# Gated delta rule in a fused two-layer kernel: keys and queries stay in the convolution's tiles, and their products move 128 columns

## The chip, the cores and the metric

The kernel runs on one core of a Trainium2 chip. The metric is the device time of one execution in microseconds, given as the median of several runs. Three runs of the kernel before gave 1481.29 us (1479.42 to 1482.24).

The core's engines run side by side, each with its own queue of instructions in order: PE (TensorE, matrix products, with its weight loads listed as PEld), DVE (VectorE), ACT (ScalarE, functions from tables that have to be loaded), POOL (GpSimd) and SP (which here only issues DMAs).

## The reference, cut to what matters

There are 1024 tokens of 256 features. Each of two layers mixes and then applies experts; the change touches only the first layer's attention, a chunked gated delta rule with 16 key heads and 32 value heads of 128:

```python
conv = silu(causal_conv(x @ w_qkv, conv_w))      # depthwise, four taps
q, k, v = split(conv)                            # q, k: 16 heads, v: 32 heads
q = l2norm(q); k = l2norm(k)
A = where(strict, -(k_beta @ k.T) * decay, 0)    # per chunk
attn = inverse(I - A)                            # unit lower triangular
...
attn_i = where(lower, q_i @ k_i.T * d_i, 0)
o_i = (q_i * exp(g_i)) @ state + attn_i @ v_new
out = rms_norm(core) * norm_w * silu(x @ w_z)
x = x + out @ w_out
```

For the change, what counts is this: after the convolution, silu is applied to keys and queries; the products of keys with keys and of keys with queries (the grams) are formed; and the squares of both are summed for the norm. Everything is float32.

## The kernel before

Tokens are handled in two halves (s = 0, 1) of two sequences of 256 tokens each. A unit is one key head with its two value heads in one half, so there are 32 units, named by head and half. Four units make a group. Inside a unit the 256 tokens of a sequence are two chunks (n = 0, 1) of 128, and b is the sequence.

A unit goes through these stages. In `Unit.products` (line 771) `convolved` (line 728) makes the projection with two products of 512 columns for q and for k, and ACT and DVE apply the four taps into a tile `accq` or `acck` of 128 x 512 (2 KB on each partition). ACT then writes silu into two new tiles, `kq0` and `kq1`, one for each chunk, with q and k of a chunk side by side: four activations of 256 elements. PE forms the grams (lines 795 to 819): for each of three pairs of chunks and each sequence, one product with k of one chunk as weights and the 256 columns of k and q of the other chunk moving. Two activations square `kq0` and `kq1`, and the products `kt` sum the squares over tokens. DMA brings the cumulated decay rows, and POOL and ACT make of them the decay matrix `attnT`, which POOL multiplies with the grams into the group's `X` and into `attnT`.

`Group.small_inverses` (line 482) then inverts the 32 x 32 diagonal blocks of a group's four units at once, mostly on DVE: transposes `Rt` of X, a chain of 60 small operations on `xs`, and the transposes `Tc` and `Rt_c`. `Unit.inverse` and `Group.inverse64` join the blocks with small products (`lu`, `lx`, `lxu`) and evictions by DVE and ACT. `Unit.values` convolves the values (`accv`, products `cvv`; silu is applied in place there), `Unit.outputs` runs the products `vn`, `at` and `ks`, `Unit.normed` normalizes and gates (POOL), and `Group.project` (`wo`) adds the projection to x for two units at a time. `Rest` holds everything after the attention, with the experts' products `h`, `a`, `e` and `ae`.

Nobody wrote the instruction order by hand. Every operation is recorded on a tape with an engine, an estimated cost, the tiles that it reads and writes, and sometimes a due time; `Tape.plan` (line 289) simulates the five engines and picks, in up to ten rounds, which operation each engine issues next. It knows how many tiles are free: nearly all tiles of 2 KB come from one pool of `PLACES` places (line 1439), and `MOST` (line 1441) limits how many each use may hold at once, with 4 where there is no entry. `SPARE` (lines 257 and 418) sets how many PSUM banks are kept for more urgent work, and `ENOUGH` (lines 287 and 423) sets when small products on PE are held back. So a change of the tiles, the costs or these numbers can change the order of all engines. Operations are emitted through one helper, so in the profile nearly all of them have line 128, and they are told apart by their tiles.

Of the kernel before, what the change touches and what calls it, by code (L numbers as in the profile page):

```python
# [11 lines left out]
AF = mybir.ActivationFunctionType  # L12
# [4 lines left out]
P = 128  # L17
B, T, C = 4, 256, 256
NTOK = B * T
NH = 16  # L20
# [161 lines left out]
class Tape:  # L182
# [11 lines left out]
    def op(self, engine, cost, emit, r=(), w=(), port=False, table=None, due=None, late=0.0, to=None, dense=1.0,  # L194
           few=False):

        o = Op()
        o.engine, o.cost, o.emit, o.late, o.table, o.due = engine, cost, emit, late, table, due
        o.dense, o.few = dense, few
        o.port = port or engine == "POOL"
        o.before, o.after, o.bufs = set(), [], []
        o.order = n = len(self.ops)
        for accesses, write in ((r, False), (w, True)):
            for at in accesses:
                buf, parts = at if isinstance(at, tuple) else (at, None)
                for other, its, wrote in buf.history:  # L210
                    if (write or wrote) and (parts is None or its is None or parts & its):
                        o.before.add(other)
                if write and parts is None:
                    buf.history.clear()
                buf.history.append((n, parts, write))
                if buf.bufs is not None and buf not in o.bufs:
                    o.bufs.append(buf)
                    buf.uses += 1
        for buf in to if isinstance(to, list) else [to] if to else []:
            if buf not in o.bufs:  # L220
                o.bufs.append(buf)
                buf.uses += 1
        o.before.discard(n)
        for i in o.before:
            self.ops[i].after.append(n)
        self.ops.append(o)
# [188 lines left out]
            o.emit()  # L415


ROUNDS, SWITCH, LOAD, SPARE, AHEAD, EACH, END, IDLE, MOMENT, GAP, RATE, GIVES = 10, 11.7, 1.3, 106.8, 160.0, 23.99, 1300.0, 54.95, 0.68, 66.3, 3.14, 5.0
UNIT = 42

EARLY, FEW = range(3, 5), 6
WIDE = 96
WINDOW, ENOUGH, LITTLE, SLOW, THIN = 3.4, 0.51, 0.38, 0.5, 10.0


def _mm(n, count=1):

    return count * {512: 0.86, 256: 0.43, 128: 0.222, 64: 0.149, 32: 0.05}[n]


def _act(n):
    return 0.2 + 0.00078 * n
# [252 lines left out]
class Unit:  # L685
# [85 lines left out]
    def products(self):  # L771
        p, s, h = self.p, self.s, self.h
        e, op = p.e, p.tape.op
        gate = p.gateb[s]
        w = self.load("wqk")

        kq = self.kq = [self.buf([P, 2, 2, P], "kq0", 2), self.buf([P, 2, 2, P], "kq1", 6)]
        for j, at in ((1, 0), (0, 1)):
            acc = self.convolved(w, at, at * NH + h, "qk"[j == 0])
            for n in range(2):  # L780

                def emit(n=n, j=j, acc=acc):
                    e.scalar.activation(
                        kq[n]()[:, :, j, :], acc()[:, :, n * P : n * P + P], AF.Silu
                    )

                op("ACT", _act(256), emit, [acc], [(kq[n], {j})], table="silu")


        kqm = []  # L790
# [3 lines left out]
        cost = lambda n: (engine, length(n))  # L794
        def gram(n0, n, ps):
            for b in range(2):
                e.tensor.matmul(
                    ps()[:, b * 256 : b * 256 + 256],
                    kq[n0]()[:, b, 0, :],
                    kq[n]()[:, b].rearrange("p j d -> p (j d)"),  # L800
                    start=True,
                    stop=True,
                )

        for pairs in (((0, 0),), ((1, 1), (0, 1))):
            of = []
            for n0, n in pairs:
                ps = p.ps(f"gram{n0}{n}_{self.tag}")
                m = self.buf([P, 2, 2, P], "kqm" if n0 == n else "cross", 2, name=n0)
                kqm.append(m)  # L810
                of.append((n0, n, ps, m))

            def grams(of=of):
                for n0, n, ps, _ in of:
                    gram(n0, n, ps)

            op(
                "PE",
                _mm(256, 2 * len(of)),
                grams,  # L820
                kq[: len(of)],
                [ps for _, _, ps, _ in of],
                to=[m for _, _, _, m in of],
            )
            for _, _, ps, m in of:

                def taken(m=m, ps=ps):
                    copy(
                        m().rearrange("p j b d -> p b j d"),
                        ps().rearrange("p (b j d) -> p b j d", b=2, j=2),  # L830
                    )

                op(*cost(512), taken, [ps], [m])
        self.cross = kqm[2]

        ps = p.ps(f"kt_{self.tag}")
        sums = lambda j: ps()[:, 504 + 4 * j : 508 + 4 * j]

        sqs = []
        for n in range(2):  # L840
            sq = self.buf([P, 2, 2, P], "sq", 2, name=n)
            sqs.append(sq)
            op(
                "ACT",
                _act(512),
                lambda n=n, sq=sq: e.scalar.activation(sq(), kq[n](), AF.Square),
                [kq[n]],
                [sq],
            )

        def norms(ps=ps):


            for at in reversed(range(8)):
                j, n, b = at // 4, at // 2 % 2, at % 2
                e.tensor.matmul(
                    ps()[:, 505 + at - WIDE : 505 + at],
                    sqs[n]()[:, b, j, :],
                    p.const(LT)[:, P - WIDE :],
                    start=True,  # L860
                    stop=True,
                )

        op("PE", 1.0, norms, sqs, [ps], dense=0.7)

        k2, ki = self.buf([P, 4], "k2", 3), self.buf([P, 2, 2], "ki", 3)
# [346 lines left out]
    def gates(self, early=False):  # L1213
# [18 lines left out]
        for n in range(2):  # L1232
            zs = self.buf([P, 2, 2, P], "zse" if early else "zs", 3, name=n)
            of.append(zs)
            ps = p.ps(f"z{n}_{self.tag}")

            def products(n=n, ps=ps):
                for b in range(2):
                    for k in range(2):
                        e.tensor.matmul(  # L1240
                            ps()[:, b * 256 : b * 256 + 256],
                            p.tokens(4 * s + 2 * b + n)[:, k, :],
                            wz()[:, k, :],
                            start=k == 0,
                            stop=k == 1,
                        )

            op("PE", _mm(256, 4), products, [wz, p.actb[s]], [ps], to=zs, few=early)

            def silu(zs=zs, ps=ps):  # L1250
                e.scalar.activation(
                    zs().rearrange("p v b d -> p b v d"),
                    ps().rearrange("p (b v d) -> p b v d", b=2, v=2),
                    AF.Silu,
                )

            op("ACT", _act(512), silu, [ps], [zs], table="silu")
# [97 lines left out]
class Program:  # L1355
# [80 lines left out]
            return self.place(tag, name, shape)  # L1436
        return Buf(self.tape, pool, shape, tag, f"{tag}_{name}", bufs)

    PLACES = 59

    MOST = {'attnT': 20, 'kq1': 12, 'kq0': 2, 'kqm': 16, 'cross': 10, 'vo': 8, 'zs': 6, 'oT': 6, 'w0': 6, 'hw0': 8, 'w1': 6, 'hw1': 8, 'wo': 2, 'sq': 4, 'r0': 5, 'wqk': 20, 'vn': 20, 'acck': 20, 'wb0': 12}

    def place(self, use, name, shape=(P, 512)):

        to = Buf(self.tape, self.up, list(shape), "place", f"{use}_{name}", self.PLACES)
        to.slots.in_turn = False
        to.slots.rate = RATE
        return to.queue(self.tape, use, self.MOST.get(use, 4))

# [3 lines left out]
    def ps(self, name):  # L1453
        ps = Buf(self.tape, self.psum, [P, 512], "ps", f"ps_{name}", 6)
        ps.slots.in_turn = False
        return ps
# [760 lines left out]
```

## Time and profile before

| | |
|---|---|
| median of three runs | 1481.29 us |
| the profiled execution | 1474.44 us, its span 1472.6 us |
| PE busy | 1388.6 us, 94% of the span, 8428 products |
| DVE, ACT, POOL busy | 1127.7, 932.7, 918.6 us |
| mean granted clock of PE | 0.981 |
| ACT table loads (line 128) | 114, of 1283 ns |
| moved by DMA | 128.60 MB, mean 87 GB/s |

A row of a group gives the operation, the tiles written and read, the shape, the count, the busy time with the mean time of one, and the idle time before with what ended it. A row of the timeline starts with the start and the length of a merged piece. Each float32 product of the program appears as two products in the records, each with a weight load. The ends of products are modelled and overlap with the next, so the time that one takes in a stream is read from start to start.

### The profile page before, as it was taken

To read this page: it belongs to the slowest core of one execution; us is meant where nothing else is said; L and a number is where in the kernel's file an instruction comes from. 1 tells how busy PE (TensorE), PEld (TensorE's weight loads), DVE (VectorE), ACT (ScalarE), POOL (GpSimd) and SP (SyncE) were. 2 spreads that over 40 slices of the span, in tenths; PEclk is the share of its full clock that TensorE was granted. 3 is DMA by queue.
4 is the path that set the end of the run, shared out by engine and by line. 5 is a ranking of instruction groups with operands and counts; after the bars stand their busy time and mean duration, and the time that the engine had idled before them with its cause. 6 is when DMAs were issued, how large, how long until landed. Compare 5 with 4: busy or idle time off the path is not lost.

```text
span 1472.6 us, 24086 instructions
## 1 busy us (share of the span) xinstructions
PE 1388.6 (94%) x8428; PEld 899.4 (61%) x8428; DVE 1127.7 (77%) x2117; ACT 932.7 (63%) x2013; POOL 918.6 (62%) x913
## 2 busy tenths in 40 slices
PE   4987899999999899999999999889999999999988
PEld 2655676876875686776687677654445644444433
DVE  7799898798698679889879989955785677785133
ACT  2688788888878888888888887733342742121220
POOL 3069859948754785985986875448643654664032
PEclk9998999999999899999999999999999999999999
DMA  6042122211120231222231223155332231658030
GB/s 213 10 136 76 47 77 87 83 46 41 59 73 29 74 98 62 66 73 72 66 110 50 65 54 94 44 165 157 107 105 83 73 126 55 188 155 245 0 115 14
DMA packets 80953, 128.60 MB, mean 87 GB/s; under 512 B 10160, under 2 KB 26288, under 8 KB 80832
## 3 DMA queue, kind: packets, MB, share of 16 engines
q1 hardware_dynamic: 79824, 125.91, 28.0%
q8 instruction: 67, 1.10, 0.3%
q10 hardware_dynamic: 1008, 1.16, 0.3%
q14 instruction: 54, 0.44, 0.1%
HBM read 121.36 MB, written 5.67 MB: 86 GB/s over the span
## 4 chain that ended last, share of the span: by engine, by line
PE 70%; DVE 15%; POOL 5%; ACT 4%; issue 3%; DMA 2%; SPq 0%; DVEq 0%; POOLq 0%; ACTq 0%
PE ps_wo L128 7%; PE ps_cvv L128 6%; PE ps_h L128 5%; PE ps_a L128 5%; PE ps_z L128 5%; PE ps_at L128 4%; PE ps_gram L128 4%; PE ps_ae L128 4%; PE ps_e L128 3%; PE ps_kt L128 3%; PE ps_cvk L128 3%; PE ps_cvq L128 3%; PE ps_vn L128 3%; DVE accv_v L128 2%; PE ps_mix L128 2%
## 5 line engine op out<-in xcount | busy, mean ns | idle before, releaser
L128 ACT ACT_TABLE_LOAD x114 | 146.3, 1283 | 21.5 <-DVE sb_xT L128 8.9
L128 DVE SCALAR_TENSOR_TENSOR accv_v<-ps_cvv,sb_convw,accv_v 128x510 f32<-128x510 f32 (+2 forms) x192 | 141.7, 742 | 7.2 <-ACT accv_v L128 2.2
L128 POOL TENSOR_TENSOR hw_h<-hw_h,r_h 128x512 f32<-128x512 f32 x64 | 85.9, 1348 | 77.7 <-DVE hw_h L128 76.1
L128 PE MATMUL ps_cvv<-ratio,wv 128*128 128x512 f32 x256 | 122.5, 609 | 2.3 <-DVE acck_k L128 1.3
L128 PE MATMUL ps_h<-ratio,w_w 128*128 128x512 f32 x256 | 117.7, 601 | 7.4 <-DMA w_w<-in_w 5.8
L128 ACT ACTIVATE r_h<-ps_h 128x512 f32<-128x512 f32 x64 | 38.2, 597 | 132.2 <-PE ps_h L128 129.4
L128 PE MATMUL ps_a<-hw_h,w_w 128*128 128x512 f32 x256 | 117.0, 595 | 1.6 <-POOL hw_h L128 1.6
L128 PE MATMUL ps_z<-wz,ratio 128*128 128x256 f32 x480 | 116.1, 390 | 0.4 <-ACT zs L128 0.4
L128 PE MATMUL ps_wo<-oT,wo 128*128 128x512 f32 x256 | 112.8, 593 | 0.8 <-ACT oT L128 0.8
L128 POOL TENSOR_TENSOR hw_e<-hw_e,r_e 128x512 f32<-128x512 f32 x32 | 41.5, 1312 | 92.1 <-ACT r_e L128 61.0
L128 PEld LDWEIGHTS ps_z<-wz,ratio 128*128 128x128 f32 x480 | 89.8, 194 | 14.2 <-issue 0.9
L128 POOL TENSOR_TENSOR vd<-vn,dc 128x512 f32<-128x512 f32 x32 | 34.1, 1064 | 98.3 <-ACT vn L128 97.8
L128 POOL TENSOR_TENSOR X<-attnT,kqm 128x512 f32<-128x512 f32 x64 | 83.6, 1314 | 12.4 <-ACT kqm L128 12.1
L128 PEld LDWEIGHTS ps_h<-ratio,w_w 128*128 128x128 f32 x256 | 48.5, 192 | 67.2 <-issue 59.8
L128 DVE TENSOR_TENSOR xs<-xs,prod 128x30 f32<-128x30 f32 (+14 forms) x240 | 81.2, 338 | 8.2
L128 PEld LDWEIGHTS ps_a<-hw_h,w_w 128*128 128x128 f32 x256 | 48.0, 190 | 61.5 <-issue 51.6
L128 ACT ACTIVATE junko<-vo 128x128 f32<-128x128 f32 x256 | 79.4, 310 | 7.3
L128 PEld LDWEIGHTS ps_wo<-oT,wo 128*128 128x128 f32 x256 | 48.1, 190 | 58.7 <-issue 53.1
L128 DVE TENSOR_TENSOR prod<-xs,Rt 128x30 f32<-128x30 f32 (+14 forms) x240 | 78.8, 328 | 6.4
L128 POOL TENSOR_TENSOR attnT<-attnT,kqm 128x512 f32<-128x512 f32 x64 | 82.6, 1303 | 1.5
L128 DVE SCALAR_TENSOR_TENSOR hw_h<-ps_h,wb_wb 128x512 f32<-128x512 f32 x64 | 43.8, 684 | 51.8 <-ACT r_h L128 39.2
L128 PE MATMUL ps_at<-vn,attnT 128*128 128x128 f32 x512 | 82.1, 276 | 0.0
(258 smaller groups left out, 3764.1 us busy)
## 6 DMA issues: line engine op xcount, KB each, us to landing
attnT<-G SPq DMA_DIRECT2D x64, 256.0 KB, 4.9
w_w<-in_w SPq DMA_DIRECT2D x64, 256.0 KB, 4.4
wb_wb<-w_rows SPq DMA_DIRECT2D x128, 128.0 KB, 3.3
wqk<-in_wqk SPq DMA_DIRECT2D x32, 256.0 KB, 2.9
wv<-in_wv SPq DMA_DIRECT2D x32, 256.0 KB, 3.6
wo<-in_wo SPq DMA_DIRECT2D x32, 256.0 KB, 3.0
qe<-G SPq DMA_DIRECT2D x32, 256.0 KB, 3.6
wz<-in_wz SPq DMA_DIRECT2D x30, 256.0 KB, 2.7
```

Of the source, the lines that this page charges most:

```text
L128: return self._tc.keep_in_program_order(f(*a, **k))
```

## The change

Silu is applied in place in `accq` and `acck`, each with one activation of 512 elements, and the tiles `kq0` and `kq1` are gone. A chunk of q or k is now a slice of such a tile; since k and q of a chunk no longer lie side by side, a gram that moved 256 columns becomes two that move 128 each, with the same weights loaded for both. The squares are taken of q and of k instead of chunk by chunk, with the same count and size, and the sums read them accordingly. The pool grows from 59 to 61 places, three uses get an entry in `MOST`, and two numbers of the planner change.

```diff
-ROUNDS, SWITCH, LOAD, SPARE, AHEAD, EACH, END, IDLE, MOMENT, GAP, RATE, GIVES = 10, 11.7, 1.3, 106.8, 160.0, 23.99, 1300.0, 54.95, 0.68, 66.3, 3.14, 5.0
+ROUNDS, SWITCH, LOAD, SPARE, AHEAD, EACH, END, IDLE, MOMENT, GAP, RATE, GIVES = 10, 11.7, 1.3, 57.48, 160.0, 23.99, 1300.0, 54.95, 0.68, 66.3, 3.14, 5.0
...
-WINDOW, ENOUGH, LITTLE, SLOW, THIN = 3.4, 0.51, 0.38, 0.5, 10.0
+WINDOW, ENOUGH, LITTLE, SLOW, THIN = 3.4, 0.53, 0.38, 0.5, 10.0
...
-        kq = self.kq = [self.buf([P, 2, 2, P], "kq0", 2), self.buf([P, 2, 2, P], "kq1", 6)]
+        kq = [None, None]
         for j, at in ((1, 0), (0, 1)):
-            acc = self.convolved(w, at, at * NH + h, "qk"[j == 0])
-            for n in range(2):
-
-                def emit(n=n, j=j, acc=acc):
-                    e.scalar.activation(
-                        kq[n]()[:, :, j, :], acc()[:, :, n * P : n * P + P], AF.Silu
-                    )
-
-                op("ACT", _act(256), emit, [acc], [(kq[n], {j})], table="silu")
+            acc = kq[j] = self.convolved(w, at, at * NH + h, "qk"[j == 0])
+            op(
+                "ACT",
+                _act(512),
+                lambda acc=acc: e.scalar.activation(acc(), acc(), AF.Silu),
+                [],
+                [acc],
+                table="silu",
+            )
+
+        def chunk(j, n, b):
+            return kq[j]()[:, b, n * P : n * P + P]
...
             for b in range(2):
-                e.tensor.matmul(
-                    ps()[:, b * 256 : b * 256 + 256],
-                    kq[n0]()[:, b, 0, :],
-                    kq[n]()[:, b].rearrange("p j d -> p (j d)"),
-                    start=True,
-                    stop=True,
-                )
+                for j in range(2):
+                    at = (2 * b + j) * P
+                    e.tensor.matmul(
+                        ps()[:, at : at + P],
+                        chunk(0, n0, b),
+                        chunk(j, n, b),
+                        start=True,
+                        stop=True,
+                    )
...
-                _mm(256, 2 * len(of)),
+                _mm(128, 4 * len(of)),
                 grams,
-                kq[: len(of)],
+                kq,
...
-        for n in range(2):
-            sq = self.buf([P, 2, 2, P], "sq", 2, name=n)
+        for j in range(2):
+            sq = self.buf([P, 2, T], "sq", 2, name=j)
...
-                lambda n=n, sq=sq: e.scalar.activation(sq(), kq[n](), AF.Square),
-                [kq[n]],
+                lambda j=j, sq=sq: e.scalar.activation(sq(), kq[j](), AF.Square),
+                [kq[j]],
...
-                    sqs[n]()[:, b, j, :],
+                    sqs[j]()[:, b, n * P : n * P + P],
...
-    PLACES = 59
+    PLACES = 61
...
-    MOST = {'attnT': 20, 'kq1': 12, 'kq0': 2, 'kqm': 16, 'cross': 10, 'vo': 8, 'zs': 6, 'oT': 6, 'w0': 6, 'hw0': 8, 'w1': 6, 'hw1': 8, 'wo': 2, 'sq': 4, 'r0': 5, 'wqk': 20, 'vn': 20, 'acck': 20, 'wb0': 12}
+    MOST = {'attnT': 20, 'kq1': 12, 'kq0': 2, 'kqm': 16, 'cross': 10, 'vo': 8, 'zs': 6, 'oT': 6, 'w0': 6, 'hw0': 8, 'w1': 6, 'hw1': 8, 'wo': 2, 'sq': 4, 'r0': 5, 'wqk': 20, 'vn': 20, 'acck': 20, 'wb0': 12, 'qe': 2, 'wv': 8, 'state': 16}
```

## The prediction

> **What bounds the kernel now.** I read the totals of the page first, then the chain of work that ended last, then busy time by stretches, then the tensor engine's timeline where a stretch was not full.
>
> ```profile
> PE 1388.6 (94%) x8428; PEld 899.4 (61%) x8428; DVE 1127.7 (77%) x2117; ACT 932.7 (63%) x2013; POOL 918.6 (62%) x913
> PEclk9998999999999899999999999999999999999999
> ...
> PE 70%; DVE 15%; POOL 5%; ACT 4%; issue 3%; DMA 2%; SPq 0%; DVEq 0%; POOLq 0%; ACTq 0%
> ```
>
> PE is the bound, and 70% of the chain is PE. The other 30% is where the change can pay or cost. Where that lies is told by busy time in stretches (columns: stretch, its length, busy us of each engine, then granted PE clock, DMA share, GB/s):
>
> ```profile
> 37.00:154.00 117.00, 96.11 (x394) 67.07 (x394) 103.32 (x216) 89.84 (x169) 70.43 (x71) 0.91 0.22 71
> ...
> 208.00:475.00 267.00, 265.43 (x2004) 193.43 (x2003) 226.65 (x438) 223.52 (x505) 184.94 (x184) 1.00 0.21 62
> 475.00:515.00 40.00, 33.00 (x289) 24.46 (x288) 26.62 (x55) 34.34 (x72) 27.95 (x30) 0.87 0.21 68
> 515.00:925.00 410.00, 405.38 (x3259) 303.44 (x3258) 356.80 (x675) 343.09 (x787) 309.78 (x310) 1.00 0.24 73
> ```
>
> From 208 to 475 and from 515 to 925 PE is full: there only PE work counts. Before 154 it is idle 21 us and slowed (clock 0.91), while DVE (103 of 117) and ACT (90) are the full engines. What PE waits for there:
>
> ```profile
> 118.41 1.89 PE L128 MATMUL ps_z<-wz,ratio 128*128 128x256 f32 x8
> 128.30 3.73 PE L128 MATMUL ps_kt<-sb_consts,sq 128*128 128x96 f32 x16 [8.00 <-ACT sq L128]
> ...
> 145.65 1.95 PE L128 MATMUL ps_cvv<-ratio,wv 128*128 128x512 f32 x4
> 154.11 1.06 PE L128 MATMUL ps_lu<-Tc,X 32*32 32x32 f32 x32 [6.50 <-DVE vo L128]
> ```
>
> 8.0 us for a square on ACT, then 6.5 us for the first group's inverse (its end, the transposes Tc and Rt_c, is named as DVE's next row). After the first wait the 16 kt passes take 3.52 us (128.30 to 131.82), against 1.76 from 89.14 to 90.90: each long wait also halves the clock for a while.
>
> **The part that is certain: 128-column products.** Each of 32 units had 6 products of 256 columns and gets 12 of 128. Every product is two passes in the records. A pass's printed duration (389 ns against 276 ns) is pipelined, so I take start to start:
>
> ```profile
> 303.44 1.89 PE L128 MATMUL ps_z<-wz,ratio 128*128 128x256 f32 x8
> 305.17 1.04 PE L128 MATMUL ps_vt<-sb_consts,accv_v 128*128 128x128 f32 x8
> ...
> 318.51 1.06 PE L128 MATMUL ps_ks<-vd,cross 128*128 128x128 f32 x8
> 319.40 1.88 PE L128 MATMUL ps_cvk<-ratio,wqk 128*128 128x512 f32 x4
> ```
>
> Eight passes of 256 columns take 1.73 us, eight of 128, each with its own weights, 0.89. A product of 256 is 0.4325 us, two of 128 are 0.445; times 192 is +2.4 us, about +2.8 with medians over the whole trace (0.1115 and 0.2157 us a pass). I take +2.8; PE is the bound, so all of it is on the path. [...] The ks row above has the very shape with a new weight each pass and spends 111 ns on load and stream together, so the load is hidden; the row decides.
>
> **Silu and squares.** The rows (all ACT; busy, mean ns):
>
> ```profile
> L128 ACT ACTIVATE accv_v<-accv_v 128x512 f32<-128x512 f32 x64 | 38.6, 626 | 1.2 <-DVE accv_v L128 0.8
> L128 ACT ACTIVATE sq<-kq 128x512 f32<-128x512 f32 x64 | 37.8, 622 | 0.3
> ...
> L128 ACT ACTIVATE kq<-accq_q 128x256 f32<-128x256 f32 x64 | 24.7, 412 | 0.5 <-DVE accq_q L128 0.4
> L128 ACT ACTIVATE kq<-acck_k 128x256 f32<-128x256 f32 x64 | 24.1, 409 | 0.8 <-DVE k L128 0.7
> ```
>
> Four of 0.41 become two of 0.626, the in-place silu that the values already have: 1.64 - 1.25 = -0.39 us a unit, -12.5 us of ACT in all; squares keep size and count. The order of the two kernels shows 115 table loads against 116, -1.3 us. Where PE is full (stretches 208 to 475, 515 to 925) this is hidden: worth 0. It counts only before 154 and at 475 to 515, where ACT is full. A gram now waits for both whole silus, not for the k and q halves of its chunk; before, the third of four was needed, so no later.
>
> **What the new order moves.** Tiles, settings and pool change the planner's whole order. I compare both orders by work ahead of a step, counted with the trace's own spacings. Three things matter.
>
> (1) From the product h27 of the first half's experts (before: about 1088 us) to the end, all five engines run the same instructions in the same order. That stretch is worth 0. DMA counts are equal (573 on SP), 64-column and smaller products too.
>
> (2) Up to the first inverse product (lu of unit 0) PE has 108.1 us of work ahead, before 97.9: +10.2 us now fill the waits above (the last grams of units 6 and 7, the values of unit 3). ACT has 95.2 against 100.4 us ahead of the first inverse's eviction, with 21 table loads against 24, so the squares that PE waited 8 us for come earlier; sq of unit 7 has 79.3 us of ACT work ahead, before 92.1. Against it: DVE has 2.7 us more ahead of Tc, and POOL 7.2 us more ahead of the last X tile (45.2 against 38.0). POOL finished that at 113.5 and DVE began its transposes at 118.4 only, so both give about the same: lu at 154.1 to 156.8, I take 156.8. Then PE's chain from lu to vn of unit 0 holds 4.7 us by the count, before 10.5. With real issue of the small products that is 7.0 us, plus what the evictions expose (rows 0.42, 0.44, 0.65, 0.57 with some 0.2 us each way, partly covered) 1.4: 8.4, or 12 if the clock is halved. Before it took 16.0 (154.1 to 170.1). So vn of unit 0 starts at 165 to 169; I take 167.
>
> Lag is time less PE work done. Before: 170.1 - 108.4 = 61.7. After: 167 - 112.8 = 54.2, so -7.5. By the first projection (work 146.4) some is given back: POOL has 2.2 us more ahead of unit 1's norm, which feeds it, in a stage where POOL is busy 42 of 50 us. I keep -5.8.
>
> (3) At 475 to 515 PE waits in small pieces (33.0 of 40 us, clock 0.87) in the fourth group's inverse. Between its lx and vn the order now puts 10.6 us of PE work, before 5.6, and ACT has 7.6 us less ahead: bounds 0 to -6, I take -2.0. Around 930 to 950 one wait (lx to lu64, 0.6 us of cover before, 12.6 after) goes and another gets thin (lu to lx, 10.7 to 2.0; at a cover of 2.0 the third group of before lost under 0.5): -0.5, bounds -3 to +2. Elsewhere PE stays full: 0, bounds +-3.
>
> The pool of 61 places and the tiles held until the grams have read them cost no instruction; the q tiles are limited to 4 (no entry), the kq0 tiles were to 2. Loads may start earlier or later; DMA share 0.2 leaves room: 0, bounds +-1.
>
> Sum: +2.8 - 5.8 - 2.0 - 0.5 = -5.5. The profiled execution took 1474.44 us (span 1472.6), so 1468.9; the median of the runs is 6.85 above, so 1475.8.
>
> **Rivals.**
> *Given back* (1481): the early gain of 5.8 shrinks to some 3 because POOL and DVE, at 90 of 100 us from 100 to 200, set the first projection; with the grams +2.8 nothing is left. For it: those two rows. Against: ACT, not they, ended the longest wait.
> *Bare chain, slower* (1487.5): DVE's 2.7 us delay all of the first inverse, and between lu and vn PE has so little to do that the clock is granted at half for some 10 us after, as in the stretch 125 to 150 (0.80 granted): 172.8 + 5.1 - 112.8 = 65.1, +3.4 of lag, +2.8 for the grams: +6.2. It decides if vn of unit 0 starts after about 170.
> [...]
> *No saving on ACT* (in-place silu waits on itself): then -3 at most is lost, 1479; accv_v at 626 ns in place speaks against it. It is part of the second case.
>
> **How the numbers follow.** Likeliest case 60%, 1475.8, own range 1467 to 1478. About no change 20%. Slower 20%, most of it the bare chain. A measurement of this kernel can tell about 0.2%, 3 us, from no change. Range 1465 to 1488: down to all bounds of (2) and (3) together, up to the bare chain.
>
> **What would show it.** Right: first lu at 154 to 157, vn of unit 0 before 169, no 8 us wait for sq, granted clock over 0.91 before 154; gram passes 111 ns apart; PE still full from 208 on; the last 385 us of equal length. Wrong: vn after 170, a new wait of over 3 us between 208 and 925, or gram passes over 130 ns apart.

## The result, and the profile after

The changed kernel takes 1492.27 us (median of 5 runs, 1491.61 to 1493.15); the kernel before, run beside it, 1482.24 (1479.42 to 1483.47). The ratio is 1.0064, interval 1.0047 to 1.008: 10 us slower, where 6 us faster was forecast. The profiled execution after took 1492.27 us (span 1490.5), its own median. The profiled execution before took 1474.44, below all five timed runs here; of the 159 timed beside the experiments, the lowest took 1474.45 and the next 1477.10. So the traces lie 17.9 us apart and the medians 10.0, and 8 us of what the traces show is not the change.

The page after, its totals, the granted clock and the chain of work that ended last:

```profile
PE 1396.2 (94%) x8812; PEld 917.6 (62%) x8812; DVE 1128.4 (76%) x2117; ACT 927.1 (62%) x1948; POOL 917.5 (62%) x913
...
PEclk9999699999999999999999999899999999999999
...
PE 77%; DVE 10%; ACT 4%; POOL 4%; DMA 3%; issue 2%; SPq 0%; ACTq 0%; DVEq 0%; POOLq 0%
```

PE is still the bound, and has a larger share of the chain than before. But the clock row has a new dip in its fifth slice (149 to 186 us) and one at about 950 us. Busy time by stretches, the same columns as before (stretch, length, busy us of PE, PEld, DVE, ACT, POOL, then the PE clock, DMA share, GB/s):

```profile
37.00:154.00 117.00, 105.62 (x526) 77.52 (x526) 98.76 (x195) 85.44 (x152) 60.48 (x63) 0.93 0.18 60
154.00:208.00 54.00, 39.34 (x526) 33.67 (x527) 49.93 (x86) 36.89 (x88) 45.89 (x46) 0.75 0.21 62
208.00:475.00 267.00, 263.60 (x2093) 195.58 (x2092) 226.89 (x440) 220.28 (x493) 187.04 (x186) 1.00 0.23 70
475.00:515.00 40.00, 36.11 (x308) 26.54 (x307) 31.37 (x71) 34.36 (x67) 23.21 (x26) 1.00 0.28 87
515.00:925.00 410.00, 403.98 (x3431) 307.17 (x3429) 343.24 (x649) 346.77 (x770) 318.60 (x316) 1.00 0.23 69
925.00:1060.00 135.00, 120.48 (x591) 68.83 (x590) 92.22 (x209) 59.47 (x134) 73.20 (x71) 0.92 0.39 113
```

and the two of them that the prediction does not show, before:

```profile
154.00:208.00 54.00, 52.90 (x601) 41.27 (x602) 47.04 (x86) 47.25 (x115) 45.56 (x44) 0.96 0.21 60
925.00:1060.00 135.00, 127.00 (x626) 71.36 (x625) 96.23 (x198) 61.59 (x136) 85.24 (x84) 0.97 0.41 122
```

What was forecast for the first stretch and for 475 to 515 came: PE does 9.5 us more before 154 at a better clock, and 475 to 515 is fuller at full clock. The loss is at 154 to 208, where PE is busy 39.34 us in place of 52.90, and in the last stretch, 120.48 in place of 127.00. The TensorE timeline after, around the first inverse (last bracket: idle time before, and its releaser):

```profile
125.27 3.53 PE L128 MATMUL ps_kt<-sb_consts,sq 128*128 128x96 f32 x16 [1.89 <-ACT sq L128]
...
163.00 1.06 PE L128 MATMUL ps_lu<-Tc,X 32*32 32x32 f32 x32 [10.23 <-DVE Tc L128]
...
174.01 3.78 PE L128 MATMUL ps_z<-wz,ratio 128*128 128x256 f32 x8 [0.61 <-DVE accv_v L128]
```

The 8.0 us wait for sq is now 1.9. But lu starts at 163.0, where it had been 154.1, after a wait of 10.2; vn of unit 0 starts at 180.4 (before 170.1); and the eight z passes take 3.78 us, twice 1.89: the clock was at half for 23.9 us from 156. And around the last inverse:

```profile
945.62 1.06 PE L128 MATMUL ps_lu<-Tc,X 32*32 32x32 f32 x32 [4.37 <-DVE Tc L128]
...
949.74 1.54 PE L128 MATMUL ps_vt<-sb_consts,accv_v 128*128 128x128 f32 x6 [2.43 <-ACT accv_v L128]
```

Before, the same product had this row:

```profile
932.40 0.69 PE L128 MATMUL ps_lu<-Tc,X 32*32 32x32 f32 x32 [0.41 <-DVE Tc L128]
```

So the wait for Tc was 0.4 us and is 4.4, and the clock is at half for 13.7 us from 944.7 (before for 3.4, from 947.1).

I use lag as in the prediction, time less PE work done at the trace's own spacings, and read it where the same amount of work is done: 200 us of work is the end of the first inverse, 400 to 500 lies around 475 to 590 us, 800 to 980 around 890 to 1095. The table has the lag that each stretch of work adds, for both kernels and for the runs told of below. The whole work is 1347.3 us before and 1350.1 in all others.

| trace | to 200 | 200-400 | 400-500 | 500-800 | 800-980 | to the end |
|---|---|---|---|---|---|---|
| before | 62.2 | 2.5 | 13.5 | 7.9 | 13.3 | 20.8 |
| e1, order of before | 69.8 | 2.2 | 13.5 | 7.4 | 15.6 | 21.2 |
| e2, order of before | 70.6 | 2.3 | 14.3 | 7.4 | 15.6 | 18.9 |
| after | 73.3 | 1.5 | 9.0 | 6.4 | 24.9 | 20.0 |
| e5, after again | 74.6 | 1.5 | 9.0 | 6.3 | 26.0 | 19.3 |
| e14, GpSimd waits | 69.5 | 1.5 | 10.6 | 6.4 | 21.9 | 22.9 |
| e17, three moves | 69.1 | 1.5 | 10.2 | 9.2 | 23.0 | 21.8 |
| e18, old order, GpSimd waits | 63.7 | 2.2 | 15.1 | 7.5 | 14.9 | 21.6 |

The row of before stands 8 us under e1 and e2 in the first column, although all three have the same order. That is the luck of the profiled execution; what it is made of, the experiments show. The row of e18 has luck of the other kind: its profiled execution is the slowest of its 19 runs.

### The profile page after: what moved, and what is told of

Its sections match the earlier page's. It is cut to its first block, busy times and chain, and to the rows that moved or that the text cites. A ratio compares the mean times of both kernels' runs of the same rounds, so it can differ in the third digit from the quotient of the medians.

```text
span 1490.5 us, 24739 instructions
## 1 busy us (share of the span) xinstructions
PE 1396.2 (94%) x8812; PEld 917.6 (62%) x8812; DVE 1128.4 (76%) x2117; ACT 927.1 (62%) x1948; POOL 917.5 (62%) x913
## 4 chain that ended last, share of the span: by engine, by line
PE 77%; DVE 10%; ACT 4%; POOL 4%; DMA 3%; issue 2%; SPq 0%; ACTq 0%; DVEq 0%; POOLq 0%
PE ps_wo L128 7%; PE ps_z L128 7%; PE ps_h L128 6%; PE ps_cvv L128 6%; PE ps_a L128 5%; PE ps_at L128 5%; PE ps_gram L128 4%; PE ps_kt L128 4%; PE ps_ae L128 4%; PE ps_vn L128 4%; PE ps_e L128 3%; PE ps_cvq L128 3%; PE ps_cvk L128 3%; PE ps_lx L128 2%; PE ps_mix L128 2%; PE ps_lu L128 2%
## 5 line engine op out<-in xcount | busy, mean ns | idle before, releaser
L128 PE MATMUL ps_cvv<-ratio,wv 128*128 128x512 f32 x256 | 118.8, 600 | 1.8 <-ACT oT L128 1.8
L128 POOL TENSOR_TENSOR vo<-vo,zs 128x512 f32<-128x512 f32 x64 | 81.7, 1297 | 0.0
```

The lines of the kernel that those rows point to most:

```text
L128: return self._tc.keep_in_program_order(f(*a, **k))
```

## The experiments

Each ran on one chip beside the kernel before; times are medians, ratios are to the kernel before, with 95% interval. For a kernel in a given order the planner's result is replaced by a written list of its steps; nothing else differs. A "diff" of such a kernel lists the steps moved, by engine.

| run | us | ratio | interval |
|---|---|---|---|
| e1 grams split | 1486.66 | 1.0006 | 0.9991-1.0021 |
| e2 code after, old order | 1483.63 | 0.9992 | 0.9979-1.0005 |
| e3 old first stage | 1494.28 | 1.0068 | 1.0055-1.0081 |
| e4 old first and last | 1491.15 | 1.0032 | 1.0012-1.0052 |
| e5 after again | 1492.42 | 1.0057 | 1.0039-1.0074 |
| e6 hs ahead | 1491.67 | 1.0052 | 1.0037-1.0068 |
| e7 filled first | 1492.46 | 1.0064 | 1.0043-1.0084 |
| e8 both | 1493.85 | 1.0067 | 1.0041-1.0093 |
| e9 DVE relieved, last | 1496.35 | 1.0082 | 1.0054-1.011 |
| e10 DVE relieved, first | 1498.9 | 1.0101 | 1.0074-1.0127 |
| e11 both | 1499.03 | 1.0102 | 1.0074-1.013 |
| e12 GpSimd waits, old order | 1483.65 | 0.9995 | 0.9981-1.0009 |
| e13 cvv10 early | 1494.57 | 1.006 | 1.004-1.008 |
| e14 GpSimd waits, new order | 1489.22 | 1.0029 | 1.0016-1.0041 |
| e15 e13 and e14 | 1491.99 | 1.005 | 1.0031-1.0069 |
| e16 old settings | 1498.51 | 1.0093 | 1.0069-1.0116 |
| e17 e15 and transposes | 1492.86 | 1.0058 | 1.0039-1.0076 |
| e18 old order, GpSimd waits for all | 1479.68 | 0.997 | 0.996-0.998 |

### Is it the edit or the order?

```diff
 e1 (kernel before)
-    matmul(ps[:, b*256 : b*256+256], kq[n0][:, b, 0], kq[n][:, b])
+    for j in range(2):
+        matmul(ps[:, (2*b+j)*P :][:, :P], kq[n0][:, b, 0], kq[n][:, b, j])
 e2 (kernel after)
-    order = planned
+    order = that of the kernel before; a pair of half silus -> one whole silu
```

> The kernel before with one edit: each product of 256 columns is issued as two of 128; tiles, silus and the order on every engine stay. Own count (0.1115 against 0.2157 us a pass): +2.8 us of TensorE work on the path, so 1485. [...] If the order alone made the loss, this run must not show more than 3 of the 10 us.

> The code after, with every step issued in the order of the kernel before (each pair of half silus becomes the one whole silu at the place of the first). Theory 'the new order costs it': products +2.8, ACT 12.5 us less, hidden for the most part, so 1485, at most 1 us under e1. Rival 'the edit costs it' (tiles held longer, grams that wait for both silus, silu in place): the loss stays, 1490 to 1494.

The splitting costs 0.9 us (-1.3 to +3.1), which holds the +2.8 counted. All of the edit in the old order costs nothing that can be told from none. So the 10 us are the new order's: 1.0064 and 1.0057 against 0.9992.

### Which stage of the order?

```diff
 e3
-    order = new
+    order = old up to the first projection + (the rest of new)
 e4
+    order = old up to the first projection + new up to lx of unit 10 + (the rest of old)
```

> The code after; what stands ahead of the first projection of the kernel before is issued in its order, all the rest in the order after. Theory: lag at the first projection back from 72 to about 62, inverse of the first group at 154, so 10 us of the 18 between the two traces go: 1482. Rival 'taken up later' (the stages that follow lose what the first one gained): 1490.

> As e3, and from the third group of the second half on (about 895 us) the order of the kernel before again. Theory: the first stage of before (lag 62), the middle of after (18 us of lag from 208 to 890, before 22) and the last inverse of before (15 us from 890 to 1060, after 25): 1475 to 1478. Rival: a piece of an order brings its gain only with the rest of it, 1485 or more.

The theory failed, and partly so did the experiment. e3's first inverse was 8 us sooner than after's (vn at 172.5), but 6 us went at once behind the seam, where two orders meet: the lag grew from 63.5 to 69.9 between 150 and 200 us of work, where neither order alone loses over 1.5. e4 lost 7 us between 700 and 800 in the same way (a wait of 3.6 us at 897). Both pieced orders paid at their seams, so what followed are single moves.

### The first stage: DVE beside GpSimd

e1's and e2's traces show why the same order gave 62 and 70. DVE adds the decay (attnT, both inputs in SBUF) in a row of 20 small instructions while GpSimd multiplies. Before, DVE and GpSimd together from some 90 us:

```profile
90.10 3.49 DVE L128 SCALAR_TENSOR_TENSOR attnT<-attnT,nG,sb_consts 128x128 f32<-128x128 f32 x13
90.63 3.87 POOL L128 TENSOR_TENSOR attnT<-attnT,c 128x512 f32<-128x512 f32 x1 [1.65 <-ACT attnT L128]
```

and e1, the same instructions of the same order, from some 92:

```profile
92.11 6.55 DVE L128 SCALAR_TENSOR_TENSOR attnT<-attnT,nG,sb_consts 128x128 f32<-128x128 f32 x7
92.37 1.24 POOL L128 TENSOR_TENSOR attnT<-attnT,c 128x512 f32<-128x512 f32 x1 [1.64 <-ACT attnT L128]
93.58 2.62 POOL L128 TENSOR_TENSOR X<-attnT,kqm 128x512 f32<-128x512 f32 x2
```

In the first, DVE does 13 additions in 3.5 us, and the GpSimd multiplication, 1.0 to 1.2 us elsewhere, takes 3.87. In the second, GpSimd runs nearly undisturbed, and of DVE's 7 additions in 6.6 us the last five take as long as one GpSimd instruction each. Both traces agree in that one engine stands still for the other; in the first GpSimd waited out eleven additions in a row. Why the one waits for the other, no trace shows. The row of 20 additions took 7.5 us before and 16.1 in e1, and Tc of the first group came at 149.8 and 157.9.

That this race falls either way with the same code in the same order is shown by e3 and e4, which are equal up to about 890 us. Their rows of the 20 additions:

```profile
87.66 7.99 DVE L128 SCALAR_TENSOR_TENSOR attnT<-attnT,nG,sb_consts 128x128 f32<-128x128 f32 x20
```

```profile
86.44 15.84 DVE L128 SCALAR_TENSOR_TENSOR attnT<-attnT,nG,sb_consts 128x128 f32<-128x128 f32 x20
```

Tc followed at 151.9 in e3 and at 157.1 in e4. Three kernels move GpSimd out of the way:

```diff
 e12 (old order), GpSimd        e14 (new order), GpSimd
+attnT_2 * c (two)              +attnT_2 * c (two)
 attnT_0 * c ... (nine steps)    attnT_1 * c, X of unit 1 (four steps)
-attnT_2 * c (two)              -attnT_2 * c (two)
 e18 (old order): DVE           GpSimd                      ScalarE
+add attnT_3 (two)              +attnT_3 * c (two)          +exp attnT_3 (two)
 taps of units 5, 6, 0           +attnT_2 * c (two)           ...
-add attnT_3 (two)               attnT_0 * c ...             -exp attnT_3 (two)
```

The forecasts for the three, should GpSimd's work be what makes the additions slow (eight take 2.2 us where it stands idle, in e1 and after): e12 at 1476 to 1479 us, with 12 to 14 us for the eight groups of additions and Tc at 150 to 152; e14 at 2 to 4 us less than e5, with Tc 3 to 4 us sooner; e18 at 1476 to 1480, with 11 to 13 us and Tc at 148 to 151. Should the additions be slow for another reason, e12 would take the time of e2 or more; should the spread of the runs come from elsewhere, e18 would have Tc sooner and a median of 1482 to 1485.

> The kernel of e2 (code after, order before) with one move on GpSimd alone: two multiplications that need the additions to attnT of unit 2 go ahead of nine that don't, so GpSimd stands still until DVE has done six of its eight additions. [...]

> The kernel after with one move on GpSimd, as in e12: the two multiplications that need the additions to attnT of unit 2 go ahead of four that don't. [...] Rival: GpSimd, standing still, is as late as before: same as e5.

> The kernel of e2 (code after, order before) with all eight additions to attnT in one row on DVE and GpSimd held until they are done: the two multiplications that need unit 3 go first on it, the two of unit 2 next, then the rest. [...]

e18's DVE row and its GpSimd row:

```profile
86.83 9.36 DVE L128 SCALAR_TENSOR_TENSOR attnT<-attnT,nG,sb_consts 128x128 f32<-128x128 f32 x28
```

```profile
97.28 6.03 POOL L128 TENSOR_TENSOR attnT<-attnT,c 128x512 f32<-128x512 f32 x6 [8.07 <-ACT attnT L128]
```

GpSimd stands still for 8 us, DVE does 28 additions in 9.4 us, Tc comes at 149.1, and the kernel takes 1479.68, 0.3% less than before and less than either kernel, with all 19 runs between 1477.1 and 1482.2 (before beside it: 1480.6 to 1488.0). Not all of this need come of holding GpSimd: e18 also does the additions of unit 3 ahead of five groups of taps, and no run has the one without the other. In the new order e14, which moves nothing but four GpSimd instructions, cut the eight groups of additions from 15.7 to 12.1 us, Tc from 162.1 to 157.3 and the median by 3.2 us against e5. e12 was a miss in the median: its trace is 5 us better than e2's (1481.14 against 1485.99 for the profiled executions), its median the same. It left the two groups of unit 3 in the race, and one took 5.8 us in its trace; that this makes the rest of the spread is not shown, since no trace shows e12's slower runs. And the race is not the whole spread: e18's runs, with no race left, still fall into two sets, 12 up to 1480.2 and 7 from 1481.5.

### The first inverse: filling it, relieving it

```diff
 e7  TensorE                          e10 DVE
-cvv of unit 3 (two) ahead of lu      -scale vo of units 0, 1 (four), one scan ahead of Tc
+cvv of unit 3 behind lu_0, lu_1      +the same behind lx_0, lu64_0
     ScalarE: their two copies too        TensorE: vt of units 0, 1 behind lu_0, lx_0
```

> The kernel after, unchanged, for a second look at how far one execution tells of the next. [...] The last inverse should be as before: a wait of 4.4 us for its first product, the clock at half for 10 to 14 us behind it. Time 1490 to 1494.

> The kernel after with the two last convolution products of the first four units (cvv of unit 3, 3.4 us, and their two copies on ScalarE) moved from ahead of the first inverse to behind its first products. Theory 'bare chain': lu comes at the same time, since DVE sets it, the wait ahead of it grows by 3.4, and the chain from lu to vn of unit 0 does 3.4 us more work in the same 17 us: 3 to 6 us less than e5. Rival 'the chain gets longer by what is put in': same as e5 or up to 3 more.

> The kernel after with DVE relieved ahead of its first inverse: the four scalings of the values of units 0 and 1 and one scan (4.2 us of DVE in all) go behind Tc of unit 0, the four transposes on TensorE that feed them behind lu of unit 0. Theory 'DVE sets the first inverse and all follows from it': Tc at 156 to 158 in place of 161 to 162, and the end 4 us sooner. Rival 'taken up later': Tc sooner, the end within 2 us of e5.

e5 repeats the trace after closely (the eight groups of additions take 15.7 us, where 13 to 20 was expected; Tc of the first group at 162.1, after 160.9; the wait at the last lu 4.4 again). e7 changed nothing: vn at 180.2, as in e5 (180.5), although the clock was back at full speed for 6.9 us of its chain. The expectation was ill thought: both places lie ahead of vn, and as long as vn's time is set by the chain, only work fetched from behind vn would count. In e10 4.2 us of DVE's work were gone and Tc came at 162.1, as in e5. None of the 4.2 us had stood where they count: some lay ahead of the transposes of X, which began at 129.3 in e10 and 130.1 in e5, with the last X tile, and that waits for the additions of unit 3. The rest lay behind the transposes, where DVE in e10 stood idle for xs, which ScalarE writes from them:

```profile
139.81 0.20 DVE L128 TENSOR_TENSOR prod<-xs,Rt 128x30 f32<-128x30 f32 x1 [2.54 <-ACT xs L128]
```

And what was moved made the chain from lu to vn 21.2 us long, not 16.3: the median rose by 6.5.

### The last inverse

```diff
 e6 TensorE                  e9 DVE                                e13 TensorE, ScalarE, DVE
+hs0, hs1                   -taps of cvv_12 among the solve       cvv_10 and z_9 exchanged,
 lu_12                       transposes Tc, Xc                     taps of cvv_10 into DVE's
-hs0, hs1                   +taps of cvv_12, cvv_13 behind         idle time ahead of X
 e8 = e6 + e7    e11 = e9 + e10    e15 = e13 + e14
 e17 = e15, and on DVE:
 transpose X (first)
+transpose X (second to fourth)
 evictions of lx_10, lu64_10, lx_11, lxu64_10 ...
-transpose X (second to fourth)
```

In e9 hs0 and hs1 take cvv_13's place ahead of lu, and cvv_13 goes behind lu and lx.

> The kernel after with two groups of products (hs0, hs1 of the experts, 4 passes each, both with operands ready since about 875 us) moved on TensorE from behind the first product of the last inverse to ahead of it. Theory 'the wait costs the clock': the wait of 4.4 us is filled with 3.4 us of work, the stretch at half clock behind it shrinks from some 12 to 3 to 7 us, so 5 to 9 us less than e5. Rival 'the wait is only moved' (the chain of the inverse sets the end, the 3.4 us are missing behind it): within 2 us of e5.

> Both moves of e6 and e7. If each works, the sum: 8 to 15 us less than e5, so about the kernel before or 3 us under it. If stages give back to each other, no better than the better of the two.

> The kernel after with DVE relieved ahead of its last inverse: the taps of both convolutions of unit 12 (4.6 us of DVE) go from among the 30 steps of the last inverse to behind its transposes, the second transpose goes straight behind the first, and TensorE does hs0 and hs1 ahead of the inverse and two cvv products behind its first ones. Theory 'DVE sets the last inverse': Tc of the last group 4.6 us sooner after Tc of the first than in e5 (778 in place of 782.6 us), the wait of 4.4 us gone, 4 to 8 us less than e5. Rival 'TensorE sets it': Tc sooner, the end within 2 us of e5.

> The moves of e9 and e10 together: 8 to 12 us less than e5 by the theory that DVE sets both inverses, so 1481 to 1484, level with the kernel before.

> The kernel after with two steps of TensorE exchanged: the two cvv products of unit 10 (second half) go ahead of the two z products of unit 9 that stand 12 us before them, with their copies on ScalarE, and DVE does their taps (4.6 us) where it stands idle at 875 to 881 us, not behind the last X tile. Theory 'DVE work left behind the last X sets the last inverse' (6.7 us more left than in the old order): from the last X to Tc 57 us in place of 61.9, the wait of 4.4 us gone, 4 to 7 us less than e5. Rival 'the stage takes its time anyway, whatever is moved' (as in e9): within 2 us of e5.

> The moves of e13 and e14 together: 6 to 11 us less than e5, so 1482 to 1486, if both theories hold.

> The kernel of e15 with one more move on DVE: the second to fourth transpose of the last group's X tile go straight behind the first (883 us), ahead of evictions of the third group for which DVE stood idle 7 us in e13 and e15. Theory 'DVE stands in order behind evictions that wait for TensorE': the four transposes take 12 us in place of 31, Tc comes 3 to 7 us sooner after the last X (55 to 59 us in place of 63.9), the wait for lu is gone, and the time is 3 to 7 us under e15. Rival: the evictions behind them come late in turn, TensorE waits for those, and the time is that of e15.

e13 and e17 moved DVE work ahead, and the wait stayed at 4.38 us (4.37 in after, 4.39 in e5). e17's DVE row of the projection that adds the units 8 and 9, and its lu on TensorE:

```profile
919.05 0.69 DVE L128 TENSOR_TENSOR sb_xT<-sb_xT,ps_wo 128x512 f32<-128x512 f32 x1 [0.66 <-PE ps_wo L128]
```

```profile
947.25 0.69 PE L128 MATMUL ps_lu<-Tc,X 32*32 32x32 f32 x32 [4.38 <-DVE Tc L128]
```

and the same DVE row of the kernel after:

```profile
917.44 0.69 DVE L128 TENSOR_TENSOR sb_xT<-sb_xT,ps_wo 128x512 f32<-128x512 f32 x1 [0.67 <-PE ps_wo L128]
```

In both, DVE stands at that addition and waits for TensorE's wo product. From there to Tc its row holds 26.13 us in after and 26.14 to 26.15 in e5, e13 and e17 (25 of the 30 steps of the solve, two scalings of ks, two groups of taps), against some 24 us of TensorE work from the product to lu. So TensorE waits for itself, by way of DVE, and whatever DVE does sooner is lost at that addition or in waits ahead of it (7 us in all between X and Tc in e13 and e17). In the old order the projection comes late in the solve: ten steps and 12.6 us in all are left behind it in e2, and lu there waits

```profile
943.91 0.69 PE L128 MATMUL ps_lu<-Tc,X 32*32 32x32 f32 x32 [0.40 <-DVE Tc L128]
```

only 0.4 us. In e9 21.85 us are left behind the addition, and the wait is gone:

```profile
943.97 0.69 PE L128 MATMUL ps_lu<-Tc,X 32*32 32x32 f32 x32 [0.29 <-DVE Tc L128]
```

What makes the wait is thus settled. What it costs is not: e6 filled it (0.5 left), and its trace has 20.8 us of lag in this stretch, after 24.9 and e5 26.0; but the median fell by 0.75 only, with intervals that overlap, and e8, with the same filling, did not fall. e9 got slower, since its chain from Tc to vn of unit 12 is 42.2 us long, not 37.1: the taps now stand in it, and TensorE waits 4.8 us for an oT that stands on ScalarE behind the silus of these taps. e11, both inverses relieved, is no better than e10. Against the 15.6 of e2, some 5 us of this stretch found no explanation that a run confirms. e15 and e17, forecast at 1486 or less and at 3 to 7 us under e15, kept the 4 to 5 us of e14 in the trace at the first inverse, but not in the median; why is open.

### Settings or tiles?

```diff
 e16 (kernel after)
-    PLACES = 61    SPARE 57.48   ENOUGH 0.53   limits for qe, wv, state
+    PLACES = 59    SPARE 106.8   ENOUGH 0.51   none
```

> The code after (tiles, silus, products of 128) with the planner's settings of before: 59 places, SPARE 106.8, ENOUGH 0.51, no limits for qe, wv and state. The planner makes a third order of it. If the loss came with the settings, 1480 to 1486; if any new order that the planner makes from these tiles is as likely to lose, 1488 to 1500. It doesn't tell the stages apart by itself; its trace does (Tc of the first group, lag between 800 and 1000 us).

The old settings make a third order of the new tiles, slower than after. So the settings alone did not make the loss; three orders of the same new tiles lie 15 us apart (1483.6, 1492.3 and 1498.5), more than the edit itself is worth either way.

## Why the prediction was wrong, by its own steps

**Products of 128, +2.8: right.** The work counted in the trace rose by 2.8 us, passes start 111 ns apart (two in 0.22 us below), and e1's interval holds it.

```profile
139.53 0.39 PE L128 MATMUL ps_gram<-accq_q,acck_k 128*128 128x128 f32 x2
139.75 0.39 PE L128 MATMUL ps_gram<-acck_k 128*128 128x128 f32 x2
```

**Silu, -12.5 us of ScalarE: mis-sized, without effect.** The rows after:

```profile
L128 ACT ACTIVATE acck_k<-acck_k 128x512 f32<-128x512 f32 x32 | 20.1, 628 | 0.7 <-DVE acck_k L128 0.7
L128 ACT ACTIVATE accq_q<-accq_q 128x512 f32<-128x512 f32 x32 | 20.1, 627 | 0.2
```

40.2 us of busy time in place of 48.8, so -8.6: instructions behind each other overlap in the records, and the prediction multiplied their durations (64 times 412 ns are 26.4 us, where its own row says 24.7 busy). In place silu takes 627 ns, as forecast, so "no saving on ACT" is out.

**(1) The tail, 0: right.** From 1100 us of work to the end the lag grew by 17.7 before and 16.9 after.

**(2) The first inverse, -5.8: the first failed step.** It measured +2.7 against e2 and +11.1 against the profiled execution before. The step that failed is "POOL finished that at 113.5 and DVE began its transposes at 118.4 only, so both give about the same: lu at 154.1 to 156.8". It counted how much work GpSimd has ahead of the last X tile and DVE ahead of Tc, and not what GpSimd waits for: the additions of unit 3, which stand in the middle of DVE's queue. Ahead of these DVE has 7.0 us more to do in the new order (89.0 against 82.0 us, waits and race taken off), among it two groups of value taps that stood behind them before. In the execution after DVE also waited 4.5 us longer on the way, 2.7 of it for ScalarE at 94.9 us, and lost 4.1 us more to the race. The additions after, and before:

```profile
120.60 2.19 DVE L128 SCALAR_TENSOR_TENSOR attnT<-attnT,nG,sb_consts 128x128 f32<-128x128 f32 x8 [0.22 <-issue]
```

```profile
105.00 4.18 DVE L128 SCALAR_TENSOR_TENSOR attnT<-attnT,nG,sb_consts 128x128 f32<-128x128 f32 x8
```

Meanwhile GpSimd stood idle:

```profile
123.94 2.04 POOL L128 TENSOR_TENSOR attnT<-attnT,c 128x512 f32<-128x512 f32 x2 [10.76 <-ACT attnT L128]
```

The last X ended at 128.9 (113.6) and Tc began at 160.9 (149.8). In e2 the old order itself lost 11.1 us to the race: the same additions began at 114.5, GpSimd stood idle 12.5 us, the last X ended at 124.4 and Tc began at 158.1. So against an execution of the old order that lost the race the new order's Tc is 3 us later, and against one that won it 11. With GpSimd held off, in part or in whole, Tc comes at 157.3 in the new order (e14) and at 152.9 and 149.1 in the old (e12, e18): the new order's own part is there with the race or without. The second half of the step, "8.4, or 12 if the clock is halved" from lu to vn, measured 17.4, with the clock at half for 23.9 us. Taking TensorE work out of the chain did not shorten it: 16.0 us with 10.5 of work before, 17.4 and (e5) 16.3 with 4.7.

**The base of the sum.** "The median of the runs is 6.85 above" was added as if spread over the run. The first stage has most of what separates that execution from others: the race went DVE's way in it, and e1 and e2, whose traces lie 12 us above it, are 7.6 and 8.4 us later there. The prediction took 154.1 and 170.1 as what the old order does; 162 and 179 is what e1 and e2 did. The row was in the trace (3.87 us for a multiplication of 1.04), and the prediction put nothing for it.

**(3) 475 to 515, -2.0: right in kind, too small.** 9.0 us of lag against 13.5 to 14.3: -4.5 to -5.3.

**(3) 930 to 950, -0.5, "bounds -3 to +2": the step with the largest miss.** It measured +9.3 against e2, +11.6 against before. The prediction read how much TensorE work covers each hop between the products of the inverse, and not when the first product can start: it put nothing for DVE, which at the projection's addition waits for TensorE and then has 26.1 us to do, while TensorE has 23.9. The wait of 4.4 us for Tc is new, about as much as TensorE had gained at 475 to 515, and the clock was at half for 13.7 us around it (6.8 in e2). Some 5 of the 9.3 us stay open, as said above.

**Sum.** Against e2, the same code in the old order: +2.7 - 0.8 - 5.3 - 1.0 + 9.3 + 1.1 = +6.0 us of lag, the distance of those two traces (1490.5 - 1484.2 = 6.3); the ratios of e5 and e2 to the kernel before say 0.0065, or 9.6. The rest of the difference is in part that e2's profiled execution took 2.4 us more than its median. Of the rivals, "bare chain, slower" had the sign, the place and its condition (vn after 170: it was 180.4), but stood at 20% and knew only the smaller half of the loss. "Given back" was right for the gain at 475 to 515, at another place than it named.

## What to carry to other kernels

When an order is compared, follow the one step that the others wait for back through every engine, and ask of each in-order queue what stands ahead of it and what that waits for; counts of work ahead of another step say nothing of it (7.0 us more ahead of the additions here, 2.7 ahead of Tc), and a queue that waits for TensorE on behalf of TensorE (a projection's addition in the middle of a solve) makes a wait that no work moved ahead can shorten. Before using a profiled execution as a base, ask where it differs from the median of the runs: a row far over its usual duration (3.87 for 1.04 us) points to a race that may fall otherwise next time. Where two engines get in each other's way like this, try holding the one that has time to spare until the other is done; here that gave 3.2 us in the new order (e14), and 4 in the old one together with earlier additions (e18, against e2).

## What the runs showed of the hardware

- In e1 the DVE additions to attnT (128x128, both inputs in SBUF), issued in a row beside GpSimd's work, fell into step with it: of 15 that start between 89.8 and 99.6 us the median took 1.12 us, one per GpSimd instruction of 1.1 to 1.3 us, where they start 0.26 us apart while GpSimd stands idle (eight in 2.2 us at 115 us), so four to five times slower. In before GpSimd waited out a row of them instead (3.87 us for a multiplication of 1.04). Which way it falls differs between executions of the same code in the same order (8.0 us for 20 additions in e3, 15.8 in e4).
- In the traces before and after the granted clock was at half in stretches of 3.4, 6.8, 10.2, 13.7 and 23.9 us, all multiples of 3.41 (the last stretch of each trace, cut by its end, aside). In after it stayed at half for seven times that from 156 us, over the wait for Tc and the chain from lu to vn behind it, although TensorE is busy 13.1 of the 19.5 us from Tc to vn of unit 0 by the profile. In e7, with two convolution products more in that chain and 16.1 of 20.0 us busy, it was back at full speed for 6.9 us of it. How much TensorE work brings it back was not measured.
